# Shifts of layer norms multiplied on GpSimd, token numbers and weights by a small load, and an exponential computed as a power

## The chip, the cores and the metric

The kernel runs on one core of one Trainium2 chip. The time is device microseconds of one execution; the figure used is the median over executions, with the lowest and the highest beside it. Engines are named as in the profile: PE is TensorE, DVE is VectorE, ACT is ScalarE, POOL is GpSimd, SP is SyncE (here it only issues transfers).

## The reference, cut to what matters

A graph layer over 6,250 nodes of 512 features is followed by a mixture of eight experts over the same rows. Only the second half is touched by the change. `N` is 6250, `D` 512, `H` 256, `E` 8 experts, `K` 2 experts for each token.

```python
edge_index = jnp.stack([src, dst])
x = x + _L0_gnn_ref(_layernorm(x, axis=-1), edge_index, ...)
x = x + _L0_ffn_ref(_layernorm(x, axis=-1)[None], ...)[0]

def _L0_ffn_ref(x, Wg1, bg1, Wg2, bg2, W1, b1, g1, be1, W2, b2, g2, be2, W3, b3):
    def _ln(x, g, b):
        m = jnp.mean(x, axis=-1, keepdims=True)
        v = jnp.var(x, axis=-1, keepdims=True)
        return (x - m) * jax.lax.rsqrt(v + EPS) * g + b
    logits = jax.nn.gelu(t @ Wg1 + bg1, approximate=False) @ Wg2 + bg2
    gates_full = jax.nn.softmax(logits, axis=-1)
    topv, topi = jax.lax.top_k(gates_full, K)
    topv = topv / jnp.sum(topv, axis=-1, keepdims=True)
    cw = jnp.sum(jax.nn.one_hot(topi, E, dtype=t.dtype) * topv[..., None], axis=1)
    h = jnp.einsum('td,edh->eth', t, W1) + b1[:, None, :]
    h = jax.nn.gelu(_ln(h, g1[:, None, :], be1[:, None, :]), approximate=False)
    h = jnp.einsum('eth,ehg->etg', h, W2) + b2[:, None, :]
    h = jax.nn.gelu(_ln(h, g2[:, None, :], be2[:, None, :]), approximate=False)
    o = jnp.einsum('eth,eho->eto', h, W3) + b3[:, None, :]
    out = jnp.einsum('te,eto->to', cw, o)
```

There are three layer norms for each row in this half: one of the token itself, and one after each of two expert layers. Each is applied as one ACT operation, scale times input plus shift, with scale = 1/sqrt(variance + EPS) and shift = -mean times scale. The two weights of a token are the softmax over its two highest logits, 1/(1+e) and e/(1+e), with e the exponential of their difference.

## The kernel before, in words

**The first 1,235 us** prepare the inputs, sum each node's neighbours by gathers on POOL and products with selection matrices on PE, and end in the sums of a batch norm. The change does not touch them.

**Tokens and groups.** From there on the 6,250 rows are 49 token tiles of 128 rows, in seven groups of seven. A token tile goes through `token_load` (SP loads it), `token_scale` (two DVE operations), `token_shift` (ACT, L828), `token_sum` (DVE: the sum, its statistics, and SP's store to the output, L835), `token_norm` (ACT, L804), `token_turn` (transposes on PE, L846), `token_gate` (PE L855 and GELU on ACT, L857) and `token_logits` (PE, L864). After a group's seventh tile the generator `route(q)` (L880 to L1050) chooses two experts for each token on DVE and gives each token two row numbers in a buffer in memory, `xs_d`, whose tiles of 128 rows hold tokens of one expert each. It runs in parts, each resumed at a fixed step. `send_one` scatters the 128 rows of a token tile to those places with an indirect DMA that POOL issues (L868). A row has `RW` = 528 numbers: 512 features, the token's number as a float (column `D`), its eight expert weights, and padding.

**Jobs.** There are 102 jobs, one for each filled tile of `xs_d`. A job is loaded by SP (L1071; before it SP reads the tile's number into a register, L1068), transposed on PE (`job_turn`, L1086), goes through two expert layers (`layer`: products L1096, bias addition on DVE L1099, statistics; `layer_norm` on ACT L804; `layer_turn`: transposes L1113 and GELU L1116 on ACT), a third product (L1125), `job_bias` (DVE, L1132), `job_weigh` (ACT, L1136: times the token's weight) and `job_out` (L1140: POOL issues an indirect DMA that adds the rows to the output at the tokens' numbers; each waits until the one before has landed).

**The order** is written out by hand. `ahead(i)` handles the first two groups' tokens, and the sends of group 0 go between them; this is the warm-up. Then `run(s, ...)` is called once a step. It advances nine jobs by one stage each, at lags of 0 to 9 steps, and up to five token tiles. The order within a step is: loads; transposes; `layer_turn`; the scatter of job s-9 and the bias of job s-8; the token's scale, shift and sum; the two lines `tprev.shifts()` and `prev.shifts()`; the norms of jobs s-2 and s-5 and of a token; `job_weigh`; the list `do` (sends and parts of the route); the two layers; `job_product`; the list `late`; the token's turn and gate; `step.scales()`. Each engine works its instructions off in this order.

**The statistics of a step** share one tile, `mv` (128 x 3 x 3: up to three norms, for each the mean, the variance and the shift). `scales()` at the end of a step adds EPS on DVE (L794) and raises to the power -0.5 on POOL (L795). `shifts()` (L799, DVE) computes -mean times scale. It is called in the step after, behind that step's token work on DVE, and the norms on ACT read its result.

**The buffers of a job.** A job's tile `xe` has four buffers. `job_turn` reads it on PE, and on DVE for two small copies of 128 x 1: `to`, the token number turned into an integer (L1081), and `cw`, the weight for this job's expert (L1082; the column is chosen by a register). Both have 14 buffers, since `job_out` reads `to` nine steps later.

**The exponential** in `route` is an ACT activation (L920). Between it and the GELUs ACT loads another function table.

Of the kernel before, what the change touches and what calls it, by code (L numbers as in the profile page):

```python
# [9 lines left out]
F32 = mybir.dt.float32  # L10
I32 = mybir.dt.int32
AF = mybir.ActivationFunctionType
OP = mybir.AluOpType
# [4 lines left out]
P = 128  # L18
EPS = 1e-5
OOB = 65536.0  # L20
# [8 lines left out]
def gnn_moe_kernel(ctx: ExitStack, tc: tile.TileContext, x, src, dst, wlT, b_l, wrT, gamma, beta,  # L29
                   wg1, bg1, wg2, bg2, w1, b1, g1T, be1T, w2, b2, g2T, be2T, w3, b3, out):  # L30
    nc = tc.nc
    N, D = x.shape
    NE = src.shape[0]
    E, _, H = w1.shape
# [54 lines left out]
    mhalf = const.tile([P, KD], F32, name="mhalf")  # L89
# [24 lines left out]
    tok = const.tile([P, NT], F32, name="tok")  # L114
# [32 lines left out]
    with ExitStack() as gnn:  # L147
# [13 lines left out]
        shift = big.tile([P, D], F32, name="shift")  # L161
# [23 lines left out]
        full, tail = divmod(NE, NC)  # L185
# [580 lines left out]
    def no_tokens(a):  # L766

        nc.vector.memset(a, 0.0)
        nc.vector.memset(a[:, D:D + 1], OOB)
        return a  # L770

    JOBS = {}

    class Step:
# [14 lines left out]
        def scales(self):  # L789
            if self.used:  # L790
                lo, hi = min(self.used), max(self.used) + 1
                assert hi - lo == len(self.used)
                self.part = self.mv[:, lo:hi]
                nc.vector.tensor_scalar(self.part[:, :, 1], self.part[:, :, 1], EPS, None, op0=OP.add)  # L794
                nc.gpsimd.tensor_tensor(self.part[:, :, 1], self.part[:, :, 1], mhalf[:, :hi - lo], op=OP.pow)  # L795

        def shifts(self):
            if self.used:
                nc.vector.scalar_tensor_tensor(self.part[:, :, 2], self.part[:, :, 0], -1.0,  # L799
                                               self.part[:, :, 1], op0=OP.mult, op1=OP.mult)  # L800
                self.used = []

    def normed(out_, in_, scale_shift):
        nc.scalar.activation(out_, in_, AF.Identity, bias=scale_shift[1], scale=scale_shift[0])  # L804
# [77 lines left out]
    def route(q):  # L882
# [33 lines left out]
            if i == 0:  # L916
                yield

        nc.vector.tensor_tensor(s[:, 2:4], s[:, 0:2], s[:, None, 0].to_broadcast([P, 2, n]), op=OP.subtract)
        nc.scalar.activation(s[:, 2:4], s[:, 2:4], AF.Exp)  # L920
        if rows(g[-1]) < P:

            nc.vector.tensor_scalar(mm[:, :, n - 1, :], mm[:, :, n - 1, :], isrow[:, 0:1], None, op0=OP.mult)
        nc.vector.tensor_add(m, mm[:, 0], mm[:, 1])
        nc.vector.tensor_copy(t2[:, :n, D], tok[:, g[0]:g[0] + n])
        nc.vector.memset(t2[:, :, D + 1 + E:], 0.0)
        yield
        pr = ps.tile([P, 2, GMAX, E], F32, name="pl")
        nc.tensor.matmul(pr[:, 0, :n], lower, m, start=True, stop=True)
        nc.tensor.matmul(pr[:, 1, :n], ones, m, start=True, stop=True)  # L930
        yield
        nc.vector.tensor_add(s[:, 0], s[:, 2], s[:, 3])
        nc.vector.reciprocal(s[:, 1], s[:, 0])
        nc.vector.tensor_tensor(s[:, 2:4], s[:, 2:4], s[:, None, 1].to_broadcast([P, 2, n]), op=OP.mult)
        nc.vector.tensor_tensor(am, mm, s[:, 2:4, :, None].to_broadcast([P, 2, n, E]), op=OP.mult)
        nc.vector.tensor_add(cw, am[:, 0], am[:, 1])
        yield
# [128 lines left out]
    def job_load(p):  # L1066
        sl, e = JOBS[p]
        at = nc.values_load(sl, engines=[SP_], min_val=0, max_val=SLOTS,  # L1068
                            skip_runtime_bounds_check_because="a tile's number, or SLOTS")
        xe = sb.tile([P, RW], F32, name="xe", bufs=4)  # L1070
        ld = nc.sync.dma_start(xe, xs_d[ds(at, 1)].rearrange("o p c -> p (o c)"))  # L1071
        tc.add_to_no_dep_group("full", ld.ins)
        XE[p] = xe

    def job_turn(p):
        xe = XE.pop(p)
        e = nc.values_load(JOBS[p][1], engines=[PE_, DVE_, ACT_], min_val=0, max_val=E - 1,
                           skip_runtime_bounds_check_because="an expert's number")
        to = sb.tile([P, 1], I32, name="to", bufs=14)
        cw = sb.tile([P, 1], F32, name="cw", bufs=14)  # L1080
        nc.vector.tensor_copy(to, xe[:, D:D + 1])  # L1081
        nc.vector.tensor_copy(cw, xe[:, D + 1:D + 1 + E][:, ds(e, 1)])  # L1082
        EV[p] = e, to, cw
        pt = ps.tile([P, KD, P], F32, name="pt", bufs=3)
        for k in range(KD):
            nc.tensor.transpose(pt[:, k, :], xe[:, k * P:(k + 1) * P], ident)  # L1086
        XT[p] = sb.tile([P, KD, P], F32, name="xT")
        nc.scalar.copy(XT[p], pt)
# [73 lines left out]
    def ahead(i):  # L1162

        def late_one(k, f):
            if i >= k:
                f(*flat[i - k])

        if i >= 3 and flat[i - 3] in tokens:  # L1170
            token_logits(*flat[i - 3])
        token_scale(*flat[i])
        if i:
            STEP[i - 1].shifts()
        late_one(1, token_norm)
# [20 lines left out]
    def run(s, prev, lo, hi, moves=False, do=(), late=()):  # L1196


        def on(lag):
            return lo <= s - lag < hi  # L1200

        step = Step()
        if moves:
            enter()
            if at(0):
                token_load(*at(0))
        loads(min(s + 4, hi))
        if on(0):
            job_turn(s)
        for i, lag in ((0, 3), (1, 6)):  # L1210
            if on(lag):
                layer_turn(s - lag, i)
        if on(9):
            job_out(s - 9)
        if on(8):
            job_bias(s - 8)
        if moves:
            if at(5):
                token_logits(*at(5))
            if at(1):  # L1220
                token_scale(*at(1))
                token_shift(*at(1))
            if at(2):
                token_sum(*at(2), step)
        tprev.shifts()
        prev.shifts()
        for lag in (2, 5):
            if on(lag):
                layer_norm(s - lag)
        if moves and at(3) and at(3) != normed_one:  # L1230
            token_norm(*at(3))
# [38 lines left out]
    with tc.manual_schedule():  # L1270
# [7 lines left out]
        for i in range(n0 + 2):  # L1278
            ahead(i)
            token_load(*flat[i + 3])  # L1280
            if i == 3:
                no = sb.tile([P, RW], F32, name="xe", bufs=4)
                nc.sync.dma_start(xs_d[SLOTS], no_tokens(no))
        token_logits(*flat[n0 - 1])
        begin(0)
        for i in range(MATH):
# [122 lines left out]
```

## Time and profile before

| what | value |
|---|---|
| median of 9 runs | 2034.51 us (2026.15 to 2040.34) |
| profiled execution, its own time | 2032.94 us |
| its span (first to last instruction) | 2031.2 us |
| granted TensorE clock over the span | 0.960 of full speed |
| graph layer and batch norm sums | up to 1235 us of the span |
| warm-up, to the steps of full length | 1235 to 1361 us |
| expert steps until the last group's sends have landed | 1361 to 1841 us |
| last part, without sends or tokens | 1841 to 2031 us |
| ACT table loads after 1235 us | 15 of 1.283 us: L920 x7, L1116 x5, L857 x3 |
| POOL power L795 | x121, 0.54 to 1.31 us, mean 0.86 |
| DVE L794 | x121, median 0.17 us |
| issue of one tile load on SP (L1071) | 0.34 us, landing after 3.1 us (median) |

How to read it: times of instructions are microseconds from the span's start. "L795 POOL" is an instruction of line 795 on that engine. In the lists of waits the columns are the total idle time in us, how often, and the longest, and the arrow names what ended the wait. In a timeline the columns are the start, the duration, engine, line, operation, output and inputs, and in brackets the idle time of that engine before it and what ended it. A row with xN stands for N instructions that follow each other.

### The profile page before, as it was taken

How to read it: one execution, taken by the hardware profiler on the slowest of the kernel's cores; microseconds unless marked ns; L12 is line 12 of the kernel's file. 1: busy time of each engine (PE TensorE's matmuls, PEld its weight loads, DVE VectorE, ACT ScalarE, POOL GpSimd, SP SyncE). 2: the span in 40 equal slices, each digit the busy share in tenths (PEclk: the TensorE clock that was granted, in tenths of full speed). 3: DMA queues.
4: the chain of work that ended last, by engine and by line, in shares of the span. 5: the costliest groups of instructions: out<-in, count | busy, mean ns of one | idle time of the engine just before them, and what ended most of it. 6: DMA issues, size and time to landing. Idle time of an engine off the chain costs nothing. (4 is left out here: it accounts for less than half of the span.)

```text
span 2031.2 us, 23976 instructions
## 1 busy us (share of the span) xinstructions
PE 1860.9 (92%) x6268; PEld 1032.8 (51%) x6268; DVE 1089.2 (54%) x2577; ACT 667.6 (33%) x1284; POOL 1216.3 (60%) x1229
## 2 busy tenths in 40 slices
PE   5878999999999999999999995588999998989993
PEld 2433444444444444444444443366767676766771
DVE  5652434334444444343344326778787878765661
ACT  3420101101010001011010114457767776655662
POOL 1427777777777777777777751434554645474443
PEclk9988999999999999999999996689999999999996
DMA  7868877778778888888888755646675767565532
GB/s 250 302 213 280 253 240 250 245 239 252 241 241 263 271 262 273 260 269 310 277 267 285 240 187 183 210 168 167 174 209 145 194 159 190 110 157 114 101 64 35
DMA packets 183185, 434.09 MB, mean 214 GB/s; under 512 B 32484, under 2 KB 38638, under 8 KB 182626
## 3 DMA queue, kind: packets, MB, share of 16 engines
q0 software_dynamic: 91040, 274.90, 47.2%
q1 hardware_dynamic: 91606, 156.69, 22.7%
q8 instruction: 56, 0.92, 0.2%
q10 hardware_dynamic: 396, 0.87, 0.1%
q14 instruction: 87, 0.71, 0.1%
HBM read 331.22 MB, written 104.20 MB: 214 GB/s over the span
## 5 line engine op out<-in xcount | busy, mean ns | idle before, releaser
L636 POOL DMA_INDIRECT xg<-xn_d,scol x832 | 795.2, 956 | 259.2 <-issue 126.4
L643 PE MATMUL pa<-xg,sel 128*128 128x512 f32 x1664 | 788.1, 596 | 19.9 <-DMA y_d<-xg 17.7
L643 PEld LDWEIGHTS pa<-xg,sel 128*128 128x128 f32 x1664 | 306.5, 190 | 363.5 <-issue 350.5
L1140 POOL DMA_INDIRECT out<-oe,to x102 | 166.5, 1633 | 168.9 <-DMA out<-oe,to 30.7
L795 POOL TENSOR_TENSOR mv<-mv,mhalf 128x2 f32<-128x2 f32 (+2 forms) x121 | 104.4, 863 | 202.2 <-DVE mv L794 196.5
L528 ACT ACTIVATE sq<-dt 128x512 f32<-128x512 f32 x49 | 29.5, 602 | 557.2 <-DVE dt L526 281.6
L1096 PE MATMUL pm<-w1s,xT 128*128 x816 | 205.1, 396 | 3.5 <-DVE hn L1099 3.5
L1125 PE MATMUL po<-w3s,hT 128*128 x408 | 198.2, 609 | 10.1 <-DVE oe L1132 10.1
L562 DVE TENSOR_REDUCE ss<-sel 128x128 f32<-128x2304 f32 x49 | 200.5, 4092 | 0.2
L432 PE MATMUL ph<-wl,xT 128*128 128x512 f32 x392 | 199.8, 592 | 0.7 <-ACT xT L427 0.7
L1096 PEld LDWEIGHTS pm<-w1s,xT 128*128 128x128 f32 x816 | 152.4, 197 | 22.9 <-DVE hn L1099 4.4
L1116 ACT ACTIVATE hT<-pt,gbe 128x128 f32<-128x128 f32 x408 | 154.1, 462 | 2.0 <-PE pt L1113 1.9
L507 DVE TENSOR_SCALAR rc<-pt 128x1 f32<-128x1 f32 x49 | 7.7, 158 | 270.6 <-PE pt L586 270.6
L804 ACT ACTIVATE hn<-hn,mv 128x256 f32<-128x256 f32 x204 | 112.0, 601 | 96.1 <-DVE mv L799 95.9
L868 POOL DMA_INDIRECT xs_d<-t,pos x98 | 103.7, 1058 | 42.3 <-issue 25.0
L556 DVE TENSOR_TENSOR sel<-jrow_p,dcol 128x2304 f32<-128x2304 f32 x49 | 124.4, 2539 | 0.0
L432 PEld LDWEIGHTS ph<-wl,xT 128*128 128x128 f32 x392 | 74.4, 190 | 94.2 <-issue 93.3
L526 DVE TENSOR_TENSOR dt<-ph,shift 128x512 f32<-128x512 f32 x25 | 17.3, 691 | 192.3 <-PE ph L432 192.3
L567 ACT ACTIVATE ag<-pa,rc 128x512 f32<-128x512 f32 x49 | 33.7, 687 | 249.0 <-PE pa L643 249.0
L524 DVE TENSOR_TENSOR dt<-ph,xo 128x512 f32<-128x512 f32 x24 | 16.6, 691 | 182.3 <-PE ph L432 182.3
L1125 PEld LDWEIGHTS po<-w3s,hT 128*128 128x128 f32 x408 | 76.4, 192 | 73.3 <-issue 52.9
L1096 PE MATMUL pm<-w2s,hT 128*128 x408 | 105.6, 381 | 0.0
(307 smaller groups left out, 2244.5 us busy)
## 6 DMA issues: line engine op xcount, KB each, us to landing
xe<-xs_d SPq DMA_DIRECT2D x102, 264.0 KB, 3.1
xg<-xn_d,scol POOLq DMA_INDIRECT x832, 3.8
d_d<-dt SPq DMA_DIRECT2D x49, 256.0 KB, 3.6
dt<-d_d SPq DMA_DIRECT2D x49, 256.0 KB, 3.9
xt<-in_x SPq DMA_DIRECT2D x24, 512.0 KB, 5.1
xn_d<-xt SPq DMA_DIRECT2D x24, 512.0 KB, 3.9
xy<-y_d SPq DMA_DIRECT2D x48, 256.0 KB, 5.6
xt<-in_x SPq DMA_DIRECT2D x48, 256.0 KB, 3.4
```

Of the source, the lines that this page charges most:

```text
L432: nc.tensor.matmul(p, xT[:, k, :], w[:, k, :], start=start and k == 0, stop=stop and k == KD - 1)
L556: nc.vector.tensor_tensor(SEL[t], jrow_p[:, None, :].to_broadcast([P, KS, P]), dcol[:, t // TG, (t % TG) * KS:(t % TG + 1) * KS, None].to_ ...
L562: nc.vector.tensor_reduce(ss, SEL[t].rearrange("p k j -> p j k"), AX.X, OP.add)
L636: nc.gpsimd.indirect_dma_start(out=xg, out_offset=None, in_=xn_d[:, :], in_offset=bass.IndirectOffsetOnAxis(ap=scol[:, t // TG, c:c + 1], ...
L643: nc.tensor.matmul(PA[t], SEL[t][:, k, :], xg, start=(k == 0), stop=(k == last))
L795: nc.gpsimd.tensor_tensor(self.part[:, :, 1], self.part[:, :, 1], mhalf[:, :hi - lo], op=OP.pow)
L804: nc.scalar.activation(out_, in_, AF.Identity, bias=scale_shift[1], scale=scale_shift[0])
L868: st = nc.gpsimd.indirect_dma_start(out=xs_d.rearrange("n p c -> (n p) c"), out_offset=bass.IndirectOffsetOnAxis(ap=at, axis=0), in_=rows_ ...
L1096: nc.tensor.matmul(pm, lhs[:, k, :], w[:, k, ds(e, 1), :].rearrange("p o h -> p (o h)"), start=(k == 0), stop=(k == kk - 1))
L1116: nc.scalar.activation(hT[:, k, :], pt[:, k, :], AF.Gelu, bias=gb[:, 2 * i + 1:2 * i + 2], scale=gb[:, 2 * i:2 * i + 1])
L1125: nc.tensor.matmul(po, hT[:, k, :], w3s[:, k, ds(e, 1), :].rearrange("p o h -> p (o h)"), start=(k == 0), stop=(k == KH - 1))
L1140: st = nc.gpsimd.indirect_dma_start(out=out[:, :], out_offset=bass.IndirectOffsetOnAxis(ap=to[:, 0:1], axis=0), in_=OE.pop(p), in_offset=N ...
```

## The change

It has three parts.

1. `Step.scales` now does everything. DVE writes -mean into the shift's column before the power; POOL adds EPS, raises to the power and multiplies the shift's column by the result. `shifts()` and its five calls are gone. ACT's norm thus waits for POOL. DVE has one operation a step instead of two, POOL three instead of one.
2. A job's tile `xe` holds only the 512 features. The other 16 numbers of each row (64 bytes) are loaded into a tile of their own, `ev`, with 14 buffers, by a second load on SP. `job_out` and `job_weigh` read `ev` directly, so the two DVE copies are gone; the token numbers are stored as integers' bits. `xe` is read by PE alone, `ev` by POOL's scatter and by ACT, which now chooses the column by a register. The tile that stands for "no tokens" is prepared in an idle row buffer (`t2s[1]`) instead of a buffer of `xe`.
3. In `route`, the exponential of the difference of the two logits is computed on POOL as e raised to that power (128 x 7), and the two weights from it as 1/(1+e) and e/(1+e) on DVE.

```diff
@@ no_tokens
-        nc.vector.memset(a[:, D:D + 1], OOB)
+        nc.vector.memset(a[:, D:D + 1].bitcast(I32), int(OOB))
...
+    euler = wts.tile([P, GMAX], F32, name="euler")
+    nc.vector.memset(euler, 2.718281828459045)
@@ class Step, scales
-                nc.vector.tensor_scalar(self.part[:, :, 1], self.part[:, :, 1], EPS, None, op0=OP.add)
-                nc.gpsimd.tensor_tensor(self.part[:, :, 1], self.part[:, :, 1], mhalf[:, :hi - lo], op=OP.pow)
-
-        def shifts(self):
-            if self.used:
-                nc.vector.scalar_tensor_tensor(self.part[:, :, 2], self.part[:, :, 0], -1.0,
-                                               self.part[:, :, 1], op0=OP.mult, op1=OP.mult)
-                self.used = []
+                mean, var, shift = (self.part[:, :, i] for i in range(3))
+                nc.vector.tensor_scalar(shift, mean, -1.0, None, op0=OP.mult)
+                nc.gpsimd.tensor_scalar(var, var, EPS, None, op0=OP.add)
+                nc.gpsimd.tensor_tensor(var, var, mhalf[:, :hi - lo], op=OP.pow)
+                nc.gpsimd.tensor_tensor(shift, shift, var, op=OP.mult)
@@ route
-        nc.vector.tensor_tensor(s[:, 2:4], s[:, 0:2], s[:, None, 0].to_broadcast([P, 2, n]), op=OP.subtract)
-        nc.scalar.activation(s[:, 2:4], s[:, 2:4], AF.Exp)
+        nc.vector.tensor_sub(s[:, 3], s[:, 1], s[:, 0])
+        nc.gpsimd.tensor_tensor(s[:, 3], euler[:, :n], s[:, 3], op=OP.pow)
...
-        nc.vector.tensor_copy(t2[:, :n, D], tok[:, g[0]:g[0] + n])
+        nc.vector.tensor_copy(t2[:, :n, D].bitcast(I32), tok[:, g[0]:g[0] + n])
...
-        nc.vector.tensor_add(s[:, 0], s[:, 2], s[:, 3])
-        nc.vector.reciprocal(s[:, 1], s[:, 0])
-        nc.vector.tensor_tensor(s[:, 2:4], s[:, 2:4], s[:, None, 1].to_broadcast([P, 2, n]), op=OP.mult)
+        nc.vector.tensor_scalar(s[:, 0], s[:, 3], 1.0, None, op0=OP.add)
+        nc.vector.reciprocal(s[:, 2], s[:, 0])
+        nc.vector.tensor_mul(s[:, 3], s[:, 3], s[:, 2])
@@ job_load
-        xe = sb.tile([P, RW], F32, name="xe", bufs=4)
-        ld = nc.sync.dma_start(xe, xs_d[ds(at, 1)].rearrange("o p c -> p (o c)"))
-        tc.add_to_no_dep_group("full", ld.ins)
-        XE[p] = xe
+        xe = sb.tile([P, D], F32, name="xe", bufs=4)
+        ev = sb.tile([P, RW - D], F32, name="ev", bufs=14)
+        for a, lo, hi in ((xe, 0, D), (ev, D, RW)):
+            ld = nc.sync.dma_start(a, xs_d[ds(at, 1), :, lo:hi].rearrange("o p c -> p (o c)"))
+            tc.add_to_no_dep_group("full", ld.ins)
+        XE[p] = xe, ev
@@ job_turn
-        to = sb.tile([P, 1], I32, name="to", bufs=14)
-        cw = sb.tile([P, 1], F32, name="cw", bufs=14)
-        nc.vector.tensor_copy(to, xe[:, D:D + 1])
-        nc.vector.tensor_copy(cw, xe[:, D + 1:D + 1 + E][:, ds(e, 1)])
-        EV[p] = e, to, cw
+        EV[p] = e, ev[:, 0:1].bitcast(I32), ev[:, 1:1 + E][:, ds(e, 1)]
@@ ahead
-        if i:
-            STEP[i - 1].shifts()
@@ run
-        tprev.shifts()
-        prev.shifts()
@@ the warm-up
-                no = sb.tile([P, RW], F32, name="xe", bufs=4)
-                nc.sync.dma_start(xs_d[SLOTS], no_tokens(no))
+                nc.sync.dma_start(xs_d[SLOTS], no_tokens(t2s[1][:, 0, :]))
...
-        STEP[n - 1].shifts()
...
-        tprev.shifts()
```

More of the change, by code (lines that the diff above doesn't have):

```diff
@@ L1069, in job_load @@
                             skip_runtime_bounds_check_because="a tile's number, or SLOTS")
-        xe = sb.tile([P, RW], F32, name="xe", bufs=4)
-        ld = nc.sync.dma_start(xe, xs_d[ds(at, 1)].rearrange("o p c -> p (o c)"))
-        tc.add_to_no_dep_group("full", ld.ins)
-        XE[p] = xe
+        xe = sb.tile([P, D], F32, name="xe", bufs=4)
[4 more added lines that the diff above has]
+        XE[p] = xe, ev
     def job_turn(p):
-        xe = XE.pop(p)
+        xe, ev = XE.pop(p)
         e = nc.values_load(JOBS[p][1], engines=[PE_, DVE_, ACT_], min_val=0, max_val=E - 1,
                            skip_runtime_bounds_check_because="an expert's number")
-        to = sb.tile([P, 1], I32, name="to", bufs=14)
-        cw = sb.tile([P, 1], F32, name="cw", bufs=14)
-        nc.vector.tensor_copy(to, xe[:, D:D + 1])
-        nc.vector.tensor_copy(cw, xe[:, D + 1:D + 1 + E][:, ds(e, 1)])
-        EV[p] = e, to, cw
+        EV[p] = e, ev[:, 0:1].bitcast(I32), ev[:, 1:1 + E][:, ds(e, 1)]
         pt = ps.tile([P, KD, P], F32, name="pt", bufs=3)
```

## The prediction

> **What bounds the kernel now.** I read the page's busy shares and slices first, then the waits, the starts of the 102 job steps on PE one by one, and the timelines of the places where a step is longer than its neighbours.
>
> ```profile
> span 2031.2 us, 23976 instructions
> ...
> PE 1860.9 (92%) x6268; PEld 1032.8 (51%) x6268; DVE 1089.2 (54%) x2577; ACT 667.6 (33%) x1284; POOL 1216.3 (60%) x1229
> ```
>
> PE is the bound on average, but the change touches no PE instruction: it can only win PE's idle time after 1235 us, where the token and expert steps run. In a full step PE starts its next tile's transposes (L1086) every 5.18 us, or 7.25 us when the step also carries a token tile (1469.79 to 1474.97; 1422.58 to 1429.87). Added up from job 7 (1361.15) to job 77 (1841.13), the steps are about 45 us longer than that. The rest is the warm-up, 1235 to 1361, and the tail from 1855.39, where each accumulating scatter of the output starts when the one before has landed: 31 steps of 5.34 us.
>
> ```profile
> POOL mv L795 <- DVE mv L794: 196.5, 68, 11.6
> ACT hn L804 <- DVE mv L799: 95.9, 58, 4.6
> DVE mv L799 <- POOL mv L795: 48.0, 31, 3.6
> PE pt L846 <- ACT t L804: 46.8, 21, 7.9
> POOL out L1140 <- DMA out<-oe,to: 30.7, 12, 4.0
> ```
>
> These rows are the waits (total, times, longest). The norm on ACT (L804) waits for the shift on DVE (L799) 58 times, and PE (L846) for the norm 21 times. The timeline shows why:
>
> ```profile
> 1495.06 0.88 POOL L795 TENSOR_TENSOR mv<-mv,mhalf 128x3 f32<-128x3 f32 x1 [0.61 <-DVE mv L794]
> ...
> 1498.50 0.68 DVE L834 SCALAR_TENSOR_TENSOR xt<-dt,xt 128x512 f32<-128x512 f32 x1
> ...
> 1500.05 0.13 DVE L799 SCALAR_TENSOR_TENSOR mv<-mv 128x3 f32<-128x3 f32 x1
> ...
> 1500.21 1.09 ACT L804 ACTIVATE hn<-hn,mv 128x256 f32<-128x256 f32 x2 [3.25 <-DVE mv L799]
> ...
> 1502.07 1.11 PE L846 MATMUL pt<-identx,t 128*128 128x128 f32 x4 [2.77 <-ACT t L804]
> ```
>
> The power was done at 1495.94, but the shift stood on DVE behind the token's scale and sum, 4.1 us. ACT lost 3.25 us and PE 2.77.
>
> **Part 1, the shift behind the power.** Removed: the DVE shift (121 at about 0.15 us); the EPS addition (0.17) becomes an early negation of the same size. Added: an addition before and a multiplication after each power on POOL. The trace has no such POOL operation. The nearest rows among POOL's groups by form (busy us, mean ns, idle before them):
>
> ```profile
> L795 POOL TENSOR_TENSOR mv<-mv,mhalf 128x2 f32<-128x2 f32 x72 | 59.7, 830 | 143.0 <-DVE mv L794 138.2 <-ACT tt L848 4.4
> ...
> L220 POOL IOTA tile_i<- 128x7 int32 x1 | 0.1, 138 | 0.0
> ...
> L1398 POOL MEMSET const-float32-1.0<- 128x1 f32 x1 | 0.1, 95 | 0.0
> ```
>
> So each is between 0.10 us (a fill without input) and 0.83 (the power, same tile and shapes). Powers of 1, 3 and 4 columns take 0.54, 0.88 and 1.04, which is 0.37 plus 0.17 a column; most of the column part should be the power. I take x = 0.35 us with its gap, a pair 0.70, and keep both ends.
>
> Gain: four group starts (jobs 13 to 14, 27 to 28, 41 to 42, 55 to 56) take 10.57, 11.63, 11.14 and 10.13 us for 7.25, together 14.5 too long. PE's idle there on the two norms is 2.74, 2.77, 2.77, 2.54 (L846) and 1.13, 1.06, 0.84, 0.84 (L1113), 14.7 in all. With the shift behind the power the norm of the fence can start at 1495.94 + 0.35 instead of 1500.21, earlier by more than PE lost. Late next is PE's product on DVE's bias addition (L1125, 0.4 each): I take **-13** (-6 to -14.5). The shifts of the same steps no longer hold DVE while POOL is busy (48.0 us, 31 times), but then ACT waits instead.
>
> Cost in the middle of groups: in three stretches the power ends after DVE is ready, so each norm is later by the pair. It reaches PE about once a stretch: 3 x 0.6 = **+1.8** (0 to 5). Elsewhere ACT is busy, or POOL stands idle (196.5 us on L794), and the pair hides; without that cover it would cost 0.70 a step.
>
> Cost in the sending phase: from 1785 to 1836 POOL runs scatter, sends, power without a break.
>
> ```profile
> 1823.11 0.75 POOL L795 TENSOR_TENSOR mv<-mv,mhalf 128x2 f32<-128x2 f32 x1
> 1824.05 1.62 POOL L1140 DMA_INDIRECT out<-oe,to  x1 [0.20 <-issue]
> 1825.98 1.02 POOL L868 DMA_INDIRECT xs_d<-t,free_i  x1 [0.30 <-issue]
> ...
> 1833.81 0.97 POOL L868 DMA_INDIRECT xs_d<-t,free_i  x1 [0.30 <-issue]
> ```
> ```profile
> 1837.37 3.23 SPq L1071 DMA_DIRECT2D xe<-xs_d  x4
> ...
> 1841.13 1.09 PE L1086 MATMUL pt<-identx,xe 128*128 128x128 f32 x4 [4.29 <-DMA xe<-xs_d]
> ```
>
> The last group's loads wait for the last send. Eight pairs stand before it, 5.6 us; POOL's pauses there (1.50, 2.34 and 1.20 before scatters, less 0.2 each) could take up 4.4. So +1.2 to +5.6: I take **+3**. One more pair before the tail's scatters, and the small loads among them: **+1**. Behind that POOL waits 2 to 4 us between scatters, which hides the pair.
>
> Warm-up: 14 sends of group 0 alternate with powers, five pairs in between, so the first loads come some 3 us later (now 1305.75) and half of that reaches PE. Against it stand fewer DVE operations from 1309 to 1349 and part 3: **0** (-4 to +5).
>
> Weighed against a rule. In the trace the shift costs DVE 0.15 us and POOL has no multiplication to compare. The Trainium skill, "GPSIMD Engine Reference", § 4.1 Engine selection, says that element-wise additions and multiplications belong on VectorE and are about twice as slow on GpSimd with two inputs; by that x would be 0.30 and the whole sum about 1.5 us lower. § 7 of the same page adds half for reads more than 8 bytes apart, as these columns are (three floats to a row); no run here shows it, and by that x is about 0.5 and the sum about -2.5.
>
> **Part 2, numbers and weights by their own load.** Removed: two DVE copies per job (L1081, L1082; 0.15 each) with their address arithmetic, after which DVE does 0.3 to 0.4 us less per step, and DVE's wait there for the tile (1.34 and 0.98 us at 1496.24 and 1503.41). Only the one step at a route's end is bound by DVE (68 to 69, 8.37 us): **-1** (-3 to 0). The tile's buffer is now freed by PE's transposes instead of L1082; SP waited 183.6 us for that, but loads run three steps ahead (only one PE wait of 4.29 us, above, is on a tile), so nothing is gained. Added: a second load on SP's queue per job, 0.34 us to issue, 64 bytes a row. Behind it on SP stand the next tile's load and the token's loads. In the four sending windows SP is in the loop from sends to scatter (L1071 waited 182.4 us for landings): 12 to 14 such steps of 0.34, half of them felt, give about +2; outside nothing. With its buffer wait (14 buffers, so it waits for a scatter three places before the one that the step issues, two steps or 10 us old, landing in 4.8) I take **+1** (0 to 2.5). If scatters fell further behind, SP would stop there.
>
> **Part 3, the exponential as a power.** Removed: seven activations (L920, 0.21) and most of 15 table loads of 1.28 us, two of them on the warm-up's chain (1283.75, 1324.9). Added: seven POOL powers of seven columns, 0.37 + 7 x 0.17 = 1.56 each (between 1.04 and 2.4), queued behind a step's scatter and before its own power. In route 0 DVE waits about 1.4 us more; in later routes the result is read a step later. Inside the warm-up's 0, and 0 (-1 to +1) after it.
>
> **The sum**: -13 + 1.8 + 3 + 1 + 0 - 1 + 1 + 0 = -7.2 us. The profiled execution took 2032.94 us (span 2031.2 and 1.7 around it), so 2025.7 there; the median of the nine runs, 2034.51, is 1.6 above that execution, so **2027.3 us**.
>
> **Rivals.**
> *POOL becomes the bound (slower).* If an addition or multiplication on POOL costs as much as the power (x = 0.8 with its gap, the pair 1.6), the sending phase costs 8 x 1.6 less 4.4, up to 12.8 without that slack, 10.5 in the middle; stretches +4.8, tail +1.9, warm-up +2, with -12 - 1 + 1 the sum is about +7, so 2041.6. The sum moves by some 31 us per us of x: zero at x = 0.58, measurably slower from 0.72. For it: rows only 0.2 to 0.3 us apart on POOL for most of 50 us; against it: fills and index ramps at 0.1 to 0.3.
> *Every early norm counts (much faster).* With x = 0.15: group starts -14.5, the longer steps at jobs 46 (1.7) and 59 to 61 (half of 6.9) -5.1, DVE -2, warm-up -4 (its norms on L799 come up to 8.1 us earlier), against +0.9 + 1 + 0.6 + 0.5: -22.6, so 2011.9. Against it: at 59 to 61 the token's load (9.5 us to landing) is late as well.
> *The start of a group is held by DVE anyway (no change).* The next layer's bias addition (L1099 at 1500.09) stands behind the same token work as L799 did; if PE then waits for it, only 6 of 13 come: -0.2, so 2034.3.
>
> **How the numbers follow.** About 0.2%, 4.1 us, is what the measurement can tell from no change: faster is below 2030.4, slower above 2038.6. Forecast 0.40 (own range 2021 to 2034; faster 0.32, same 0.07, slower 0.01); POOL bound 0.27 (slower 0.24, same 0.03); every norm 0.13 (faster); held by DVE 0.20 (same 0.13, slower 0.05, faster 0.02). Faster 0.47, same 0.23, slower 0.30. The range of 2013 to 2044 leaves out about half of the fastest case and the upper third of the slowest.
>
> **What would show it.** Right: waits of L804 on the shift gone or put on POOL's multiplication and below 60 us in total; the four group starts near 7.6 us; POOL's addition and multiplication rows near 0.3; one to three table loads. Wrong: rows of 0.5 us and more; the last send later than 1838 while the group starts are shorter; group starts still over 9 us, with PE idle on DVE (L1099); a later start of the first tile's transposes (1311.01), which would mean that the warm-up's sends matter more than I allow.

## The result and the profile after

The changed kernel takes 2042.65 us (median of 20 runs, 2039.41 to 2047.58), the kernel before 2031.0 (62 runs, 2022.83 to 2040.56). The ratio is 1.0058, with a 95% interval of 1.0047 to 1.0069: 0.58% or 11.7 us slower. The forecast was 2027.3 us and faster; the range of 2013 to 2044 holds the time, the sign is wrong. (Ratios here compare executions within 1.5% of the fastest of their kernel; where a session spread by 2%, that leaves some out.)

The profiled execution after took 2046.66 us. Its busy times, and then its waits:

```profile
PE 1859.8 (91%) x6268; PEld 1026.9 (50%) x6268; DVE 1052.3 (51%) x2253; ACT 648.6 (32%) x1263; POOL 1295.8 (63%) x1478
```
```profile
ACT hn L803 <- POOL mv L800: 126.1, 68, 4.0
POOL mv L798 <- DVE mv L787: 94.6, 51, 6.1
...
PE pt L845 <- ACT t L803: 54.6, 30, 10.6
```

DVE does 37 us less. POOL does 79.5 us more. The norm's wait (95.9 us in 58 places for the shift on DVE) became 126.1 us in 68 places for the multiplication on POOL; PE's wait for a token's norm went from 46.8 to 54.6 us. POOL's own waits for statistics halved (196.5 to 94.6), so its queue was full more often.

The span also holds a graph stage that was 5.1 us longer (the batch norm's copy, L745, at 1238.9 instead of 1233.8). That stage is the same code, and it varied between 1233.8 and 1240.7 among the kernels in the sessions in which the kernel before took 2031 to 2039 us, whatever the edit. So stages are compared from L745 on, in starts of PE's tile transposes; the last column ends with the start of the last scatter. Each number below is from one profile; the kernels of the other rows are told further down. Profiles of one kernel differ by up to 7 us in a stage (a third one of part 1 with EPS on DVE had 198.7 in the 24 steps, for 191.9 and 191.7) and by up to 14 in all, so the verdicts come from the timed runs, and the table only says where to look.

| from L745 on, us | to job 13 | four group starts | 24 steps behind them | jobs 62 to 79 | scatters 70 to 101 | all |
|---|---|---|---|---|---|---|
| before, two profiles | 163.5, 163.2 | 43.5, 42.0 | 184.7, 183.6 | 109.0, 107.6 | 165.4, 169.6 | 787.0, 787.7 |
| changed | 168.8 | 37.4 | 190.1 | 110.7 | 168.2 | 795.9 |
| part 2 alone | 161.3 | 41.4 | 187.0 | 106.9 | 172.1 | 788.1 |
| part 3 alone | 164.0 | 43.3 | 180.4 | 109.0 | 170.8 | 789.5 |
| part 1 alone | 166.2 | 33.5 | 198.7 | 112.5 | 171.0 | 804.1 |
| part 1, steps only | 165.8 | 34.1 | 192.2 | 111.8 | 171.9 | 799.1 |
| part 1, third operation | 168.0 | 38.9 | 190.5 | 113.9 | 167.8 | 802.2 |
| part 1, EPS on DVE, two | 162.2, 161.9 | 31.1, 30.9 | 191.9, 191.7 | 108.7, 109.3 | 166.5, 170.0 | 782.5, 787.0 |
| early shift on DVE | 166.2 | 31.5 | 189.4 | 106.4 | 171.0 | 786.3 |
| early shift, small load, two | 161.7, 166.3 | 33.8, 36.1 | 191.1, 191.7 | 107.9, 109.0 | 167.7, 172.9 | 781.5, 795.3 |
| changed, EPS on DVE | 165.2 | 37.3 | 189.3 | 108.3 | 175.3 | 797.0 |
| early shift, loads late, two | 165.3, 164.3 | 31.9, 32.5 | 180.7, 182.3 | 107.9, 106.1 | 170.8, 172.0 | 778.3, 779.4 |
| loads late alone | 161.3 | 42.3 | 176.6 | 109.4 | 170.2 | 781.1 |
| changed, loads late | 166.3 | 38.4 | 180.4 | 110.9 | 175.4 | 794.0 |
| part 1, EPS on DVE, loads late | 165.0 | 30.9 | 180.3 | 110.7 | 168.8 | 779.3 |

"Four group starts" are the steps to jobs 14, 28, 42 and 56; "24 steps behind them" the six after each (15 to 20, 29 to 34, 43 to 48, 57 to 62), in which the next group's rows are sent. In the changed kernel the starts win 5 us against the mean of the two profiles before (7.57, 9.84, 10.06 and 9.97, for 10.57, 11.63, 11.14 and 10.13 in the first of them), and the steps behind lose 6. That is little beyond the spread: parts 2 and 3, which alone are no slower than before, have 187.0 and 180.4 there. What PE waits for is clearer. In the 24 steps it stood 12.5 us waiting for a token's norm (L803), for 5.0 and 8.2 in the two profiles before; at the four starts 7.9, for 10.8 and 11.2. So the wait was moved from the starts into the steps with sends, more than it was taken away.

What a GpSimd operation costs, from POOL's groups by form after:

```profile
L799 POOL TENSOR_TENSOR mv<-mv,mhalf 128x2 f32<-128x2 f32 x72 | 53.5, 743 | 6.0
L798 POOL TENSOR_SCALAR mv<-mv 128x2 f32<-128x2 f32 x72 | 30.5, 424 | 70.6 <-DVE mv L787 70.5
...
L800 POOL TENSOR_TENSOR mv<-mv 128x2 f32<-128x2 f32 x72 | 14.9, 207 | 5.6
...
L919 POOL TENSOR_TENSOR gs<-euler,gs 128x7 f32<-128x7 f32 x7 | 10.9, 1550 | 17.1 <-DVE gs L918 12.7 <-DVE t L925 4.5
```

An addition and a multiplication take 0.63 us together, 0.32 each. The forecast's 0.35 was right as a duration. In the queue they cost more. One step of the last sends after, on POOL:

```profile
1841.75 1.65 POOL L1137 DMA_INDIRECT out<-oe,ev  x1 [0.69 <-ACT hn L803]
...
1846.33 0.97 POOL L867 DMA_INDIRECT xs_d<-t,free_i  x1 [0.30 <-issue]
1847.32 0.26 POOL L798 TENSOR_SCALAR mv<-mv 128x2 f32<-128x2 f32 x1
1847.67 0.72 POOL L799 TENSOR_TENSOR mv<-mv,mhalf 128x2 f32<-128x2 f32 x1
1848.47 0.19 POOL L800 TENSOR_TENSOR mv<-mv 128x2 f32<-128x2 f32 x1
1849.35 1.64 POOL L1137 DMA_INDIRECT out<-oe,ev  x1 [0.69 <-ACT hn L803]
```

and the same step before:

```profile
1829.26 1.62 POOL L1140 DMA_INDIRECT out<-oe,to  x1 [0.20 <-issue]
...
1834.80 0.75 POOL L795 TENSOR_TENSOR mv<-mv,mhalf 128x2 f32<-128x2 f32 x1
1835.74 1.62 POOL L1140 DMA_INDIRECT out<-oe,to  x1 [0.20 <-issue]
```

Scatter to scatter with three sends it is 7.60 us, for 6.48 before. From the end of the last send to the scatter it is 2.05 us for 0.96. The pair costs 1.1 us there: 0.45 of execution, two gaps of 0.08 to 0.09, and the scatter, which starts 0.88 us after the multiplication's start although that is over in 0.19.

Why the starts stayed long: the start of job 28 after, where the statistics of the step before were ready at 1505.4.

```profile
1504.96 0.41 DVE L797 TENSOR_SCALAR mv<-mv 128x3 f32<-128x3 f32 x1
...
1505.67 0.99 POOL L867 DMA_INDIRECT xs_d<-t,pos  x1 [0.31 <-issue]
...
1506.66 0.28 POOL L798 TENSOR_SCALAR mv<-mv 128x3 f32<-128x3 f32 x1
...
1507.03 1.28 POOL L799 TENSOR_TENSOR mv<-mv,mhalf 128x3 f32<-128x3 f32 x1
...
1508.39 0.55 POOL L800 TENSOR_TENSOR mv<-mv 128x3 f32<-128x3 f32 x1
...
1508.97 1.09 ACT L803 ACTIVATE hn<-hn,mv 128x256 f32<-128x256 f32 x2 [2.89 <-POOL mv L800]
...
1510.83 0.66 PE L845 MATMUL pt<-identx,t 128*128 128x128 f32 x4 [1.83 <-ACT t L803]
```

The sends hold POOL until 1506.66, and the three operations end at 1508.94, 3.6 us after DVE was done. In the kernel before the power there had started 0.15 us after DVE. The norm no longer stands behind DVE's token work; it stands behind POOL's sends and a chain of 2.3 us. It starts 3.6 us after DVE was done, for 5.3 before (1494.91 to 1500.21), which is about what this start won.

### The profile page after: what moved, and what is told of

Read it like the earlier page. It is cut to its first block, busy times and chain, and to the rows that moved or that the text cites. A ratio compares the mean times of both kernels' runs of the same rounds, so it can differ in the third digit from the quotient of the medians.

```text
span 2044.9 us, 24510 instructions
## 1 busy us (share of the span) xinstructions
PE 1859.8 (91%) x6268; PEld 1026.9 (50%) x6268; DVE 1052.3 (51%) x2253; ACT 648.6 (32%) x1263; POOL 1295.8 (63%) x1478
## 5 line engine op out<-in xcount | busy, mean ns | idle before, releaser
L1137 POOL DMA_INDIRECT out<-oe,ev x102 | 167.4, 1641 | 173.7 <-ACT hn L803 34.6
L803 ACT ACTIVATE hn<-hn,mv 128x256 f32<-128x256 f32 x204 | 112.0, 599 | 126.3 <-POOL mv L800 126.1
L867 POOL DMA_INDIRECT xs_d<-t,pos x98 | 106.1, 1082 | 37.5 <-issue 29.2
L1129 DVE TENSOR_TENSOR oe<-po,b3s 128x512 f32<-128x512 f32 x102 | 70.5, 691 | 83.3 <-DMA out<-oe,ev 31.4
L1122 PEld LDWEIGHTS po<-w3s,hT 128*128 128x128 f32 x408 | 77.2, 193 | 70.7 <-issue 53.6
L798 POOL TENSOR_SCALAR mv<-mv 128x2 f32<-128x2 f32 (+2 forms) x121 | 50.8, 420 | 95.0 <-DVE mv L787 94.6
```

The costliest lines, as they stand in the source:

```text
L867: st = nc.gpsimd.indirect_dma_start(out=xs_d.rearrange("n p c -> (n p) c"), out_offset=bass.IndirectOffsetOnAxis(ap=at, axis=0), in_=rows_ ...
L1122: nc.tensor.matmul(po, hT[:, k, :], w3s[:, k, ds(e, 1), :].rearrange("p o h -> p (o h)"), start=(k == 0), stop=(k == KH - 1))
L1129: nc.vector.tensor_add(oe, OE[p], b3s[:, ds(e, 1), :].rearrange("p o h -> p (o h)"))
L1137: st = nc.gpsimd.indirect_dma_start(out=out[:, :], out_offset=bass.IndirectOffsetOnAxis(ap=to[:, 0:1], axis=0), in_=OE.pop(p), in_offset=N ...
```

## The experiments

**Each part alone.** From the kernel before: part 1 (the diff of `scales` and of the five calls), part 2 (the load and its uses), part 3 (the lines of `route`). The fourth run moves two lines of the kernel before:

```diff
         if on(8):
             job_bias(s - 8)
+        tprev.shifts()
+        prev.shifts()
         if moves:
...
-        tprev.shifts()
-        prev.shifts()
         for lag in (2, 5):
```

> Part 1 alone: EPS addition, power and multiplication on GpSimd, no shift on DVE; loads and exponential as before. My theory now: the two extra GpSimd operations cost about 1.1 us a step wherever the GpSimd queue is full (in the profile after, a step of the last sends takes 6.32 us for 5.21), and nearly all of the loss is here: +6 to +10 us against before, with the group starts 1 to 3 us shorter each. Rival A: the loss comes from the small loads (part 2), and part 1 is worth what the group starts give: -4 to -8 us. Rival B: the 5 us that the graph stage was longer in the profile after belongs to the change: then the stage ends near 1239 here as well.

> Part 2 alone: token numbers and weights by a 64-byte load of their own, no copies on DVE; norms and exponential as before. My theory: +2 to +4 us, all of it in the tail, where the scatters' period went from 5.34 to 5.43 us over 31 steps in the profile after; nothing or a small gain before 1841 us. Rival A (the small loads carry the loss): +8 to +12 us. A third reading, that the tail's longer period comes from the GpSimd operations of part 1: 0 to -2 us here, and a period of 5.34.

> Part 3 alone: the exponential of the routes as a power on GpSimd. My theory: the first route is later by some 1.5 us (DVE waited 1.64 us for it in the profile after), against two table loads of 1.28 us that leave the warm-up's chain; 0 to +2 us. Rival: without table loads ACT is free earlier in the warm-up and at the group starts: -2 to -4 us.

> The kernel before with one move: the two lines that call shifts() in a step stand right behind the bias of job s-8, ahead of the token's scale and sum, so that DVE computes the shift before the token work; nothing on GpSimd changes. If the wait of the norm for the shift behind the token's work is what the long group starts are made of, the four group starts fall from 10.1 to 11.6 us to about 8, and the time by 6 to 12 us. Rival: DVE, which then waits for the power in order, holds the bias of the next layer (L1099) instead, and the starts stay over 9.5 us: 0 to -3 us, or slower by up to 3 where the power is late.

| run | ratio to before (95% interval) |
|---|---|
| part 1 alone | 1.0054 (1.0038 to 1.0070) |
| part 2 alone | 0.9991 (0.9978 to 1.0004) |
| part 3 alone | 1.0003 (0.9988 to 1.0018) |
| early shift on DVE | 1.0006 (0.9996 to 1.0017) |

Part 1 carries the loss; parts 2 and 3 cannot be told from nothing. The expected tail of part 2 is not shown: its scatters were 5.55 us apart, but those of the other three kernels as well (5.51 or 5.52). The longer graph stage is no part of the change (1238.6 in part 1 alone, but 1240.7 later in a kernel that is faster and lacks the change).

The early shift is the telling one. It does exactly what the forecast wanted from part 1, with nothing added on POOL: the starts fall to 8.00, 7.76, 7.95 and 7.80 us, 10.5 to 12 us less in all. And the time does not move. Some 5 us went in the 24 steps behind (189.4 for 184); the rest went in the warm-up (2.8) and the tail (3.5), by no more than those stages vary. PE's waits, before and then with the early shift:

```profile
PE po L1125 <- DVE oe L1132: 10.1, 14, 2.0
PE pm L1096 <- DVE hn L1099: 3.5, 3, 2.2
```
```profile
PE pt L846 <- ACT t L804: 34.7, 20, 8.3
PE po L1125 <- DVE oe L1132: 17.9, 27, 2.1
PE pm L1096 <- DVE hn L1099: 11.4, 10, 2.9
```

PE waits 12.1 us less for the token's norm (34.7 for 46.8), but 15.7 us more for DVE's two bias additions (L1132, L1099). DVE now waits for the power in order, with the additions behind it. At the four starts these waits are 5.7 us, for 1.0 and none in the two profiles before, and in the 24 steps behind again 5.7, for none before. This is the rival of that expectation, a bias held on DVE: not enough to keep the starts long, but about as much as the steps behind lost. It is read from waits; no run took it away alone.

**How many operations on GpSimd, and a second profile of before.** The edits of part 1 alone:

```diff
# EPS on DVE
-                nc.gpsimd.tensor_scalar(var, var, EPS, None, op0=OP.add)
+                nc.vector.tensor_scalar(var, var, EPS, None, op0=OP.add)
# third operation
                 nc.gpsimd.tensor_scalar(var, var, EPS, None, op0=OP.add)
+                nc.gpsimd.tensor_scalar(shift, shift, 1.0, None, op0=OP.mult)
```

> The kernel before once more, for a second profile of it beside the others. The four kernels that were run since all have scatters 5.51 to 5.55 us apart in the tail, against 5.34 in the first profile of the kernel before, though three of them are no slower. If that is the chip or the execution, this profile has about 5.5 as well, and starts its scatter of job 70 about 615 to 618 us after the batch norm sums instead of 621.6. If 5.34 is the kernel's own, every one of the three parts and the moved shift lengthens the tail.

> Part 1 alone with EPS added on DVE as in the kernel before: GpSimd has two operations a step (power, multiplication) instead of three, DVE two. Part 1 alone was 11 us slower. If the cost is what each further operation adds to GpSimd's queue (about 0.55 us of the 1.1 of the pair), this is 4 to 7 us slower. If the cost is that the norm waits for GpSimd at all, it stays at 9 to 12. If only the addition was costly, it is within 2 us of before.

> Part 1 alone with one more operation on GpSimd a step: the shift's column multiplied by 1.0 before the power, which changes no value. By the queue theory 15 to 19 us slower than before, in line with two and three operations. If the cost does not go by the operations, 10 to 12 as part 1 alone.

> Part 2 with the early shift of the run before (shifts() right behind the bias, ahead of the token work), nothing added on GpSimd. The early shift alone made the four group starts 7.8 to 8.0 us and won nothing in total. If DVE, which now waits in order for the power, gave the gain back, the 0.3 to 0.4 us a step that part 2 takes off DVE bring 3 to 6 us. If the tail's scatters or the sends set the end instead, the time stays within 2 us of before.

These ran in a session in which the graph stage took 190 to 207 us longer and the kernel before 2228 us, with a spread of 2%. From L745 on the kernel before took 787.7 us there, as in the first profile, and its scatters were 5.47 us apart: the 5.34 of the first profile was that execution. EPS on DVE measured 1.0009 (0.9976 to 1.0043), the third operation 1.0123 (1.0073 to 1.0173), the early shift with the small load 1.0026 (0.9987 to 1.0066). Three further operations are clearly slow, though by how much is open: over all executions the medians are 0.8% apart (2246.14 and 2228.07). One is not told from none here. The early shift gains nothing with part 2's copies off DVE either. That doesn't clear DVE: part 2 takes away copies, not the wait for the power, and PE waited 12.7 and 12.1 us for the two bias additions here as well.

**One line back, again, and SP's order.** In the steps behind a group start scatters wait for the token's own store. In the profile of part 1 alone, in time order:

```profile
1518.91 0.34 SPq L1068 DMA_DIRECT2D xe<-xs_d  x1
...
1519.34 0.38 SPq L832 DMA_DIRECT2D out<-xt  x1
...
1522.27 0.19 POOL L798 TENSOR_TENSOR mv<-mv 128x3 f32<-128x3 f32 x1
...
1526.81 1.66 POOL L1137 DMA_INDIRECT out<-oe,to  x1 [4.35 <-DMA out<-xt]
```

The store stands on SP behind the load of a tile, the load waits until sends have landed, the scatter on POOL waits until the store has landed, and the next sends stand behind the scatter: a loop through two queues and two landings. POOL had been done at 1522.46 and stood 4.35 us. The fourth run cuts SP's part of it, on top of the early shift:

```diff
-        loads(min(s + 4, hi))
+        if loaded <= s:
+            loads(min(s + 4, hi))
...
                 token_sum(*at(2), step)
+        loads(min(s + 4, hi))
```

> The run with EPS on DVE again (part 1 with power and multiplication on GpSimd, EPS added on DVE), since the chip of the last runs spread by 2% and left it open. On that chip its token and expert part, from the batch norm sums on, took 782.5 us, against 787.7 for before and 804.1 for part 1 alone. Theory: of the two operations that the change adds on GpSimd, the addition alone turns a gain into the loss; so 3 to 6 us faster than before. Rival (single profiles differ by that much): within 2 us of before, or slower by 4 to 7 as half of part 1 would be.

> The early shift on DVE with the small load again, 781.5 us from the batch norm sums on in one profile against 787.7: 3 to 6 us faster than before. Rival: the early shift alone was not faster and the small load alone 2 us at most, so together within 2 us.

> The changed kernel with one line back: EPS added on DVE, all else as changed. If the addition on GpSimd is what makes the change slow, this is faster than before by 3 to 8 us, so 14 to 19 us faster than the changed kernel. If the whole pair or the wait for GpSimd is, it stays slower by 3 to 8.

> The early shift on DVE, and SP's loads of a step's tile put behind the token's store of the same step (a step's loads stay first where the step needs them at once). In all profiles with short group starts (31 to 34 us for four, against 42 to 43) the six steps behind each start are longer (189 to 199 us in all, against 184). Theory: there the scatter waits for the token's store, which stands on SP behind a load that waits for the last sends to land, so what the start wins the sends lose; with the store first, those 24 steps fall to 174 to 182 us and the time by 6 to 12. Rival: they are long because GpSimd's queue of scatter, sends and power is, so nothing changes, or the loads come later and it is slower by up to 5.

Measured, in another session that spread by 2%: EPS on DVE 0.9977 (0.9932 to 1.0022), early shift with the small load 1.0021 (0.9978 to 1.0063), the changed kernel with EPS on DVE 1.0056 (1.0018 to 1.0094), early shift with loads late 0.9955 (0.9915 to 0.9995). The first was not faster by 3 to 6 us, and the third not faster at all: both expectations missed. In the third only the addition was taken back from GpSimd, and a loss of 0.18 to 0.94% stayed. The last is faster, with the 24 steps at 180.7 us for 189.4, as expected of the loop. Its waits show the cut. SP and POOL with the early shift alone:

```profile
SPq L1071 <- DMA xs_d<-t,pos: 170.3, 31, 13.1
SPq L835 <- DVE xt L834: 118.3, 28, 14.1
```
```profile
POOL out L1140 <- DMA out<-xt: 14.0, 9, 2.4
```

and with the loads late (the second run of it, below):

```profile
SPq L835 <- DVE xt L834: 246.1, 49, 14.0
...
SPq L1071 <- DMA xs_d<-t,pos: 52.3, 15, 13.6
```
```profile
POOL out L1140 <- DMA out<-xt: 2.5, 3, 0.9
```

SP's wait for the sends' landing falls from 170.3 to 52.3 us, and it now waits in front of the store for DVE instead. The scatters' wait for the store goes from 14.0 to 2.5.

**The loop in the changed kernel, and the warm-up.** The same edit in the changed kernel, in the kernel before alone, once more with the early shift, and part 1 in `run` only (the warm-up keeps EPS and shift on DVE):

> The changed kernel with SP's loads put behind the token's store, as in the run before. If the sends are a loop of scatter, store, load and landing on SP and GpSimd, which the two further GpSimd operations stretch, cutting SP's part of it takes the 24 steps behind the group starts from 190 us (changed kernel) to about 181, and the kernel is 5 to 10 us faster than the changed one: +2 to +6 us against before. Rival: the loss lies in the warm-up and the last sends alone, and the time stays at +9 to +12.

> The kernel before with the loads behind the store and nothing else. The store is then early, but the shift still stands behind the token work on DVE, so the four starts stay at 42 to 43 us; the 24 steps behind them fall from 184 to 176 to 181: 3 to 8 us faster. If only both edits together win (a gain at the starts that the sends gave back, and now do not), this is within 2 us of before.

> Early shift and late loads once more, on the chip of this call: 0.45% faster with an interval of 0.05 to 0.85% on a chip that spread by 2%. 6 to 11 us faster than before if the two edits free what the starts and the sends lost (starts 32 us, sends 181 us in its profile).

> Part 1 in the steps alone: the warm-up keeps EPS and shift on DVE, with one power on GpSimd between the sends. In the profile of part 1 alone the tokens' and experts' part was 17 us longer than before, 3 of it by job 13, and 6 in that of the changed kernel. So 2 to 5 us less than part 1 alone: 6 to 9 us slower than before. Rival: the warm-up's delay is made up later anyway (the sends of the first groups set the pace), and it stays 10 to 12 slower.

| run | ratio to before (95% interval) |
|---|---|
| changed, loads late | 1.0022 (1.0007 to 1.0038) |
| before, loads late | 0.9972 (0.9958 to 0.9986) |
| early shift, loads late | 0.9963 (0.9952 to 0.9974) |
| part 1, steps only | 1.0056 (1.0039 to 1.0074) |

With the loads late the changed kernel is 0.22% slower than before instead of 0.58%, and its 24 steps fall to 180.4. But the kernel before wins nearly as much by the same edit, and its steps fall to 176.6. With the loads late in both, the medians of 12 executions in one session are 2042.00 and 2031.56: the change still costs 10.4 us, for 11.7 without the edit. So the loop through SP costs each of these kernels 0.3 to 0.4%, and it is not what makes the change slow. Nor did scatters wait longer for the store in the changed kernel (6.0 us, for 6.8 and 5.2 in the two profiles before).

Leaving the warm-up as it was brings nothing that can be told: 11 us slower, between 8 and 15, where I expected 6 to 9. The early shift adds nothing to the late loads (2031.95 and 2031.56): the gain is the loop's alone. Its starts are 10 us shorter (32.5 for 42.3), but the steps behind again take back half (182.3 for 176.6). There PE waits 4.0 us for DVE's bias addition L1132 (3.3 in the other profile), and not at all with late loads alone.

**One operation less, with the loads late.**

> Part 1 with EPS on DVE and with the loads behind the store. Part 1 with EPS on DVE had four starts of 31 us and 192 us for the 24 steps behind them in both profiles; with the store first the latter should fall to about 181, so starts and sends together to 212 as with the early shift and late loads, and the time 6 to 10 us below before. Rival: the further GpSimd operation shows in the last sends and the tail, and the gain is 2 to 4 us.

> Part 1 with EPS on DVE once more, for an interval on a chip that spreads less: two earlier results of it were +0.09% (-0.24 to 0.43) and -0.23% (-0.68 to 0.22). If the one addition on GpSimd makes the loss of part 1 (0.54%), this is between -6 and +2 us of before; if each operation on GpSimd costs its half, +4 to +7.

Measured 0.9960 (0.9929 to 0.9990), with starts and steps at 211.2 us as expected, and 1.0004 (0.9970 to 1.0038) for part 1 with EPS on DVE. The three results of the latter, weighted by their intervals, make 1.0000 (0.9979 to 1.0021). So part 1 with one further GpSimd operation can't be told from before (over all executions the three medians are -0.16, +0.30 and +0.33% from it); with two it costs 0.54%; with three 1.23%, or 0.8% over all executions, which is not safely more than with two. In part 1, then, it is the addition on GpSimd that makes the loss. That the cost goes by the number of operations isn't shown: the third one is of the addition's kind (a tile and a number), the multiplication takes two tiles, and no run adds a second multiplication.

The best kernels of the study are early shift with loads late (0.37% faster than before) and the one with EPS on DVE and loads late (0.40%, wider interval); they can't be told apart, nor from the late loads alone (0.28%).

## Why the prediction was wrong, step by step

- **The group starts, -13 us: wrong, and the step that decided the sign.** "The norm of the fence can start at 1495.94 + 0.35" took POOL to be as free as it was in that one step. After the change the power stood behind sends there, and the starts won 5 us (9 in part 1 alone). More important, PE's idle there was counted as time of the whole. The early shift won 10.5 to 12 us at the same starts and nothing in total (1.0006, at best 0.8 us). The rival "held by DVE anyway" named a wait that the early shift does meet: PE lost on DVE's bias additions about what it had won on the norm. In the changed kernel DVE computes no shift; there PE's wait for the norm went into the steps with sends, and the total is not the 2034.3 of that rival.
- **Middle of groups, +1.8: mis-sized, if anything.** The three stretches lie in the 24 steps behind the starts. These became 6 us longer in the changed kernel (14 and 8 in the two profiles of part 1), about as much as PE's wait for the norm grew there. The sum priced the pair among sends only for the last group. The 21 steps between, without sends, are no longer than before (118.2 us for 119.7 and 120.3).
- **The pair, 0.70: mis-sized.** 1.1 us in a full queue, since the gaps and the late start of the next scatter were left out; the executions were right.
- **Last sends, +3, and the tail's start, +1: about right.** Jobs 62 to 79 became 2.4 us longer after (about 4 in both profiles of part 1), the way to scatter 70 about 1 more.
- **Warm-up, 0: too low in the profile, not settled in the time.** The first load came 78.2 us after L745, for 72.0 and 70.1: 6 to 8 later, not 3. The 14 sends with five pairs between them took 28.1 us for 22.4, so 1.1 a pair. The stage was 5.4 us longer; but it varied from 161.3 to 166.3 among kernels without any of this, and part 1 without the warm-up lost just as much.
- **Part 2, 0 in all: right in total.** One wait was larger than allowed for. SP waited for scatters before it could fill `ev`, 84.0 us in 33 places after (63.4 of it from 1860 on, where scatter follows scatter) and 73.3 in 30 in part 2 alone. Alone it costs nothing that can be measured.
- **Part 3, 0: right.** The power took 1.55 us (1.56 forecast), DVE waited 1.6 us for the first (1.4), and of the 15 table loads one was left, a GELU's at the start of the warm-up.
- **The rival "POOL becomes the bound"** gave 2041.6 with 0.27. That its time is the measured one is luck: its price of 0.8 an operation is not what was measured (0.32), and its starts won 12.

Three of the prediction's signs of being wrong came: the last send stands at 1846.33, past 1838 even without the 5.1 us of the graph stage, while the starts are shorter; three of the four starts are still over 9 us; and the first transposes come 80.9 us after L745, for 77.2 and 75.9. In the profiles the change loses 8.5 us from L745 on: +5.4 to job 13, -5.3 at the starts, +5.9 in the 24 steps, -1.8 in the 21 between, +3.6 from job 62 to scatter 70, +0.7 behind.

**What stays open.** That part 1 carries the loss is shown by runs; that it does so because the norm stands behind POOL's sends is read from PE's waits in single profiles, and no run took that wait alone away. Why the addition costs some 11 us in part 1 and the multiplication nothing isn't known. The changed kernel with EPS on DVE was still 0.56% slower (0.18 to 0.94) in a session of wide spread, though part 1 with EPS on DVE, part 2 and part 3 are each at zero. With parts 1 and 2 together the four starts took 37 to 38 us, for 31 to 34 with part 1; but the third operation, without part 2, had 38.9 as well.

The rule of the Trainium skill that the prediction weighed ("GPSIMD Engine Reference", § 4.1 Engine selection) gives a multiplication of two inputs on GpSimd about twice VectorE's time. Measured are 0.21 us against 0.15 for the DVE shift, 1.4 times. The addition has one input, for which the rule says roughly line rate; it took 0.42 against 0.17. As a price of the pair the rule was good enough. It speaks of one instruction, and in the queue of the last sends the pair of 0.45 us cost 1.1.

## What to carry to other kernels

Time that an engine stands idle in one place is worth something only if the next steps don't lose it again: ask who waits once the stall is gone, on every queue that the new order holds back. The smallest edit that takes away just the stall answers this before a larger change is built; here it was two moved lines, and they won nothing. Test a fix with and without the change: the late loads looked like the cure of the changed kernel until the kernel before won nearly as much by them. A cheap operation moved to a queue that issues DMAs costs its gaps and the next issue's delay, and it stands behind every issue that is ahead of it. Where a queue mixes loads that can wait with stores that others wait for, try their order: it won 0.28% here.

## What the runs showed of the hardware

- The same addition on 128 x 1 took between 0.22 and 0.79 us on GpSimd (1253.13 and 1243.37 in the profile after), the multiplication 0.19 to 0.73. No run told what the long ones wait for.
- In the last four steps of sends after, the scatter began 0.88 to 0.90 us after the start of a multiplication of 0.19 us; before, 0.94 after the start of a power of 0.75. The profile names ACT's norm as the releaser of the 0.69 us between. In the warm-up a send begins 0.74 us after the start of a multiplication of 0.19 or 0.30 us (1305.40 to 1306.14, 1309.53 to 1310.27), with "issue" as the reason. In all ten profiles that have a multiplication of under 0.25 us right ahead of a DMA issue, the least from its start to the issue is 0.74 us for a send and 0.78 to 0.79 for a scatter. It looks as if a DMA issue can't follow a GpSimd operation's start more closely, however short that is; no run was made for it.
- Sessions differ by 9% in the time of the kernel before, and the difference lies in one stage: up to the batch norm's copy 1234 to 1241 us in some and 1414 to 1451 in others, while from there on the kernel before takes 787.0 and 787.7. The record lists one chip number for a session of each kind, so it isn't shown that the chip makes the difference.
